# Index look-ups of 1024 columns, placed by a running count of two engines' work, in a fused attention and feed-forward kernel

## The chip, the cores and the metric

The kernel runs on one core of a Trainium2 chip. The metric is the device time of one execution in microseconds (us). Five engines work at the same time, each through its own queue in order: TensorE (PE), VectorE (DVE), ScalarE (ACT), GpSimd (POOL) and SyncE (SP). SP, ACT and POOL also issue DMA transfers.

## The reference

The input x has 2 x 2048 rows of 512 numbers. Two sublayers follow each other, each with a layer norm in front and a residual sum behind.

```python
q, k, v = x @ Wq, x @ Wk, x @ Wv             # attention between the 512 features, not the rows
w = softmax(q.T @ k / 4)                     # 512 x 512 for each of the two batches
x = x + (w @ v.T).T @ Wo                     # (x here stands for the normed x)

gate = x @ lut[gate_idx].T                   # 1376 x 512 weights, each one of 16 numbers
up   = x @ lut[up_idx].T
x = x + (silu(gate) * up) @ lut[down_idx].T
```

The weights of gate, up and down are given as indices 0 to 15 into a table of 16 numbers, and have to be looked up on the chip.

## The kernel before

All products are in float32. PE runs them in six stages one after the other: the Gram matrices of the normed x (L467), the 512 x 512 matrix chain of the attention with Strassen-like products of halves (L620), the product y of every 128 rows with that chain (L783), gate and up (L1008, tiles `a_g`, `b_g`, `c_g`, `w_g`, `x_g`, `z_g`), the last 96 of the 1376 rows (L1286), and down (L1008, tiles `a_d`, `b_d`, `c_d`). The order of PE, ACT, DVE and SP is the order of the program's text; a scheduler places the POOL instructions alone.

**Gate and up.** The 1376 hidden rows are eleven tiles `f` (0 to 10, the last has 96 rows). Every tile from 0 to 9 is multiplied with four pairs `p` of 512-column chunks: a `GateUp(f, p)` is one unit. From f = 2 on, units go by a `role`: `2 * (f % 2) + p % 2`, since products of two neighbouring tiles and two neighbouring pairs share work. A unit's stages on PE are `a1`, `c1`, `a2`, `c2`, `b`, `a3` and `a4`; `Line.run` runs the unit's `a4` late, inside the next unit. The PSUM tiles `a` and `c` have two buffers, the others one. Of a unit of role 2 (odd f, even p), DVE's last reading of the tile `a` is the addition in `a4` that makes `h1`; the unit after next begins with `a1` in the same buffer.

**The left sums.** For every even f, before the second pair's products, DVE makes sums of 128 columns of the weights of f and f + 1 (`sums_left`, tiles `lc`, `lb`, `ld`, four additions each).

**The look-ups.** A `Job` looks up 512 columns of indices: `fetch` loads them (POOL queue, two buffers), `cast` copies them to 16 bits on ACT, and `ops` runs 19 DVE instructions: three tests of a bit in 16 bits (L271, L272, L277), one shift of the indices (L275), eight picks between two table entries (L285) and seven `copy_predicated` that merge them by the bits (L297). There are 33 jobs: gate, up and down, eleven each. `ops` is a generator that yields an estimated cost after each instruction. `pump(us)` takes steps from it until the given time is spent, and is called at fixed places between PE's stages (`between`), in gate and up with a time that depends on the role:

```python
pace[0] = {0: 0.85, 1: 1.4, 2: 1.0, 3: 0.6}.get(u.role, 1.07)
```

Finished gate and up tiles are followed by four additions of 256 columns (`of_both`). Down's weights stay in SBUF in `wd` (the first six tiles) and `wd2` (the other five, which are looked up while PE already runs down's first part).

## Time and profile before

| | |
|---|---|
| median of 3 runs | 1064.85 us (1064.7 to 1065.43) |
| the profiled execution, its own time | 1064.8 us |
| its span in the profile | 1063.0 us |
| granted clock of TensorE, mean | 0.999 |
| instructions | 11592 |
| busy PE, DVE, ACT, POOL | 1057.0, 837.3, 385.0, 105.4 us |
| moved by DMA | 189.07 MB |

"Busy" is the time in which an engine ran at least one instruction. A record of a matmul is longer than the distance to the next matmul, since they are pipelined: matmuls of 512 columns have records of 592 ns and start 429 ns apart, and a float32 product has two of them. "Idle before, releaser" in a group or a line is the time for which an engine stood still ahead of an instruction, and what ended it.

### The profile page before, as it was taken

The page shows a single profiled execution, that of the slowest core. Times are in us where ns is not written, and L with a number is a line of the kernel's source. Part 1 is how long each engine was busy: PE and PEld are TensorE (multiplying, and loading weights), DVE is VectorE, ACT ScalarE, POOL GpSimd, SP SyncE. Part 2 cuts the span into 40 slices and gives each one's busy share as a digit, 9 for nine tenths or more (in the row PEclk, how much of TensorE's full clock was granted, in tenths as well). Part 3 has the DMA queues.
Part 4 walks back from the last instruction along what each step waited for, and adds up shares of the span by engine and source line. Part 5 has one row for each costly group of instructions (what it writes and reads, how often), then busy time and mean ns, then how long its engine had stood idle before and what let it go on. Part 6 is the DMA issues. An engine that isn't in the chain of part 4 may idle for free.

```text
span 1063.0 us, 11592 instructions
## 1 busy us (share of the span) xinstructions
PE 1057.0 (99%) x3554; PEld 661.0 (62%) x3554; DVE 837.3 (79%) x1842; ACT 385.0 (36%) x741; POOL 105.4 (10%) x160
## 2 busy tenths in 40 slices
PE   9999999999999999999999999999999999999998
PEld 5668887444444444444444444444998888888887
DVE  7878778889985889899699999964549998656554
ACT  4652532455532234444443444444223322211111
POOL 0000000011110120230041023013000000000000
PEclk9999999999999999999999999999999999999999
DMA  8750314499661365795597679569546675666773
GB/s 341 240 170 11 85 27 100 110 237 224 163 183 50 119 238 189 176 218 184 186 206 197 216 165 225 182 196 198 151 119 226 200 232 175 200 199 205 228 217 124
DMA packets 127710, 189.07 MB, mean 178 GB/s; under 512 B 18832, under 2 KB 59024, under 8 KB 126752
## 3 DMA queue, kind: packets, MB, share of 16 engines
q1 hardware_dynamic: 74528, 100.17, 29.9%
q0 software_dynamic: 15776, 39.92, 17.7%
q10 hardware_dynamic: 37344, 48.24, 14.0%
q8 instruction: 28, 0.46, 0.2%
q14 instruction: 34, 0.28, 0.1%
HBM read 108.60 MB, written 79.69 MB: 177 GB/s over the span
## 4 chain that ended last, share of the span: by engine, by line
PE 91%; DVE 4%; ACT 2%; DMA 1%; issue 1%; ACTq 1%; SPq 0%; DVEq 0%
PE a_g L1008 22%; PE a_d L1008 14%; PE y L783 10%; PE c_g L1008 8%; PE c_d L1008 7%; PE rows L1286 4%; PE b_d L1008 4%; PE x_g L1008 4%; PE z_g L1008 4%; PE w_g L1008 3%; PE b_g L1008 2%; PE ea_t L620 1%; PE ea_p L620 1%; PE ea_m L620 1%; DVE st_a L161 1%; PE gp L467 1%
## 5 line engine op out<-in xcount | busy, mean ns | idle before, releaser
L783 PE MATMUL y<-m,nT 128*128 128x512 f32 x256 | 110.2, 592 | 0.0
L783 PEld LDWEIGHTS y<-m,nT 128*128 128x128 f32 x256 | 48.6, 190 | 60.4 <-issue 57.4
L1008 PE MATMUL a_g<-xT_a,s 128*128 128x512 f32 x160 | 75.5, 594 | 0.0
L1008 PE MATMUL a_g<-xb,wg 128*128 128x512 f32 x160 | 75.3, 593 | 0.0
L1008 PE MATMUL c_g<-xb,wu 128*128 128x512 f32 x160 | 75.2, 592 | 0.0
L1008 PE MATMUL a_d<-dT,hs_a 128*128 128x256 f32 x288 | 72.6, 379 | 0.0
L467 PE MATMUL gp<-xn_a 128*128 128x128 f32 (+3 forms) x256 | 70.1, 434 | 0.7 <-ACT xn_a L239 0.7
L467 PEld LDWEIGHTS gp<-xn_a 128*128 128x128 f32 x256 | 43.9, 190 | 28.2 <-issue 15.1
L1008 PEld LDWEIGHTS a_d<-dT,hs_a 128*128 128x128 f32 x288 | 54.5, 189 | 7.7
L297 DVE COPY_PREDICATED wd<-b_wd,wd 128x512 f32<-128x512 int16 (+1 forms) x77 | 56.3, 732 | 1.3
L1008 PE MATMUL a_g<-xT_sq,s 128*128 128x512 f32 x120 | 56.7, 595 | 0.0
L1474 ACT COPY p_d<-a_d 128x256 f32<-128x256 f32 x32 | 11.9, 372 | 120.3 <-PE a_d L1008 120.3
L1008 PEld LDWEIGHTS a_g<-xb,wg 128*128 128x128 f32 x160 | 30.2, 190 | 38.8 <-issue 33.2
L1008 PEld LDWEIGHTS a_g<-xT_a,s 128*128 128x128 f32 x160 | 30.1, 190 | 38.9 <-issue 36.4
L1008 PEld LDWEIGHTS c_g<-xb,wu 128*128 128x128 f32 x160 | 30.4, 190 | 38.3 <-issue 38.0
L143 DVE TENSOR_TENSOR r<-r,p_d 128x256 f32<-128x256 f32 x64 | 26.9, 421 | 28.2 <-ACT p_d L1474 17.4
L285 DVE TENSOR_SCALAR wd<-idx_wd,lut_x,lut_sb 128x512 int32<-128x512 int32 (+1 forms) x88 | 45.9, 539 | 0.0
L1063 ACT COPY u<-a_g 128x512 f32<-128x512 f32 x40 | 23.4, 585 | 62.0 <-PE a_g L1008 59.6
L143 DVE TENSOR_TENSOR u<-c_g,u 128x512 f32<-128x512 f32 x40 | 27.5, 688 | 21.0 <-PE c_g L1008 15.5
L143 DVE TENSOR_TENSOR r<-r,a_d 128x256 f32<-128x256 f32 x64 | 26.6, 416 | 20.6 <-PE a_d L1008 20.6
L1286 PEld LDWEIGHTS rows<-last,xb 128*128 128x128 f32 x256 | 41.7, 190 | 0.5 <-issue 0.5
L1286 PE MATMUL rows<-last,xb 128*128 128x192 f32 x256 | 41.8, 326 | 0.0
(345 smaller groups left out, 2207.9 us busy)
## 6 DMA issues: line engine op xcount, KB each, us to landing
hd<-h SPq DMA_DIRECT2D x80, 256.0 KB, 3.3
h<-hd SPq DMA_DIRECT2D x40, 512.0 KB, 6.1
nl<-nd SPq DMA_DIRECT2D x32, 256.0 KB, 5.7
xnd<-xn_f ACTq DMA_DIRECT2D x16, 512.0 KB, 5.4
fl<-xnd POOLq DMA_DIRECT2D x32, 256.0 KB, 6.4
xn_back<-xnd SPq DMA_DIRECT2D x32, 256.0 KB, 3.8
rd<-r SPq DMA_DIRECT2D x32, 256.0 KB, 3.3
r<-rd SPq DMA_DIRECT2D x32, 256.0 KB, 4.0
```

The source lines that it names most:

```text
L143: nc.vector.tensor_tensor(dest, a, b, ALU.add)
L161: nc.vector.bn_stats(st, block)
L285: vec.tensor_scalar(dest.bitcast(I32), idx, lut_x[:rows, k : k + 1], lut_i[:rows, at : at + 1], ALU.bitwise_and, ALU.bitwise_xor,)
L297: vec.copy_predicated(dest, masks[level - 1], t)
L467: nc.tensor.matmul(gp[b][i][:, i * P :], xn[:, i, j % 2, :], xn[:, i:, j % 2, :], start=c % CPB == 0 and j == 0, stop=c % CPB == CPB - 1 a ...
L620: nc.tensor.matmul(ps[:, m, :], self.a[a][:, k, m * P : (m + 1) * P], self.b[b][:, k, :], start=first and m == k == 0, stop=k == 1, skip_g ...
L783: nc.tensor.matmul(ys[k], nTs[k][:, i, :], m[:, i, :], start=(i == 0), stop=(i == KB - 1))
L1008: nc.tensor.matmul(ps, lhsT, rhs, start=first and i == 0, stop=i == len(pairs) - 1, skip_group_check=not first,)
L1063: nc.scalar.copy(self.u2, self.a)
L1286: nc.tensor.matmul(ps[:, jj, :], x[:, j * P : (j + 1) * P], w, start=i == 0, stop=i == len(pairs) - 1,)
L1474: nc.scalar.copy(p1, self.a)
```

## The change

- A job looks up up to 1024 columns: gate and up of one tile together (`pair_job`), and two tiles of down together (`down_job`). There are 17 jobs in place of 33. The indices have one buffer in place of two; the fetch of the next job stands after the sixteenth step of a job (`LEAVES`, its last reading of the indices), and the cast of the next job after its last step.
- All of down's weights are looked up before PE starts down; each result is written to DRAM (`wdd`, on SP's queue) and read back: the first six tiles into two free rooms at the start of the stage of the last rows, the other five at the start of down.
- The weights of gate and up have four buffers in place of three (`w`), their sums three in place of two (`s`), the moving sums `tt` eight in place of nine.
- In gate and up, the last rows and down, a `Clock` adds up at build time the PE time of the matmuls and the DVE time of the additions; `fill(lead)` takes look-up steps until DVE's count is `lead` us ahead of PE's (1.4 in gate and up, 0.7 in down, -0.5 ahead of `a4` in a unit of role 3). In the stages ahead of gate and up, `pump` stays.
- The left sums of f = 4, 6 and 8 are made in the unit before, (f - 1, 3), one of the three tiles at each `between`. For role 2, the addition of `w_g` to `y` moves from `a4` to `first`.

The matmuls, their operands' values and their order are the same. The core of the diff:

```diff
+    class Clock:
+        pe = dve = 0.0
+        def matmul(self, cols):
+            self.pe += (4 * cols / 2.4 + 5) / 1000
+        def vector(self, cols, *of):
...
+            self.dve += 0.15 + 1.05 * cols / 1000
...
     class Job:
         def fetch(self, queue=nc.gpsimd):
-            self.idx = gub.tile([P, 512], I32, tag="idx", name=f"idx_{self.name}", bufs=2)[
...
+            t = gub.tile([P, 2, 512], I32, tag="idx", name=f"idx_{self.name}", bufs=1)
+            self.idx = self.part(t)
+            for i, of in enumerate(self.loads):
+                queue.dma_start(self.idx[:, i, :], of)
...
+        def after():
+            nc.sync.dma_start(wdd[:rows, i : i + k, :], made[0])
+            yield 0.1
...
             for k, cost in enumerate(job.ops()):
                 yield cost
-                if k == 9 and i + 1 < len(jobs):
-                    jobs[i + 1].cast()
-            if i + 2 < len(jobs):
-                jobs[i + 2].fetch()
+                if k == LEAVES and i + 1 < len(jobs):
+                    jobs[i + 1].fetch()
+            if i + 1 < len(jobs):
+                jobs[i + 1].cast()
+                yield 0.9
+
+    LEAVES = 15
...
+    def fill(lead):
+        while clock.dve < clock.pe + lead:
+            cost = step()
+            if cost is None:
+                clock.dve = max(clock.dve, clock.pe)
+                return
+            clock.dve += 1.1 * cost
...
         def first(self):
...
+            if self.role == 2:
+                add(self.y, of_d.ps, self.y)
...
             u.a2()
-            self.between()
             if role == 3:
+                self.between(-0.5)
                 last_a4()
+            else:
+                self.between()
...
         if sums_of and sums_of[0][0].ready(sums_of[0][1] | 1):
             next_sums_left()
         elif todo:
             todo.pop(0)()
-            pump(0.3)
-        else:
-            pump(pace[0])
+        fill(leads[0] if lead is None else lead)
...
-        if f > 1 and f % 2 == 0 and p == 0:
+        if (f, p) == (2, 0):
             sums_of += [(o, f) for o in seconds]
-        while p and sums_of:
+        if 2 < f < NFT - 2 and f % 2 and p == NPR - 1:
+            sums_of += [(o, f + 1) for o in seconds]
+        while f % 2 == 0 and p and sums_of:
             next_sums_left()
...
+    for q, (tag, n) in enumerate((("sq1", 4), ("a3", 2))):
+        t = room(tag, f"wd_{tag}")[:, :n, :]
+        nc.sync.dma_start(t, wdd[:, 4 * q : 4 * q + n, :])
...
+                nc.sync.dma_start(wd2[0][:, : NFT - K1 - 1, :], wdd[:, K1 : NFT - 1, :])
+                nc.sync.dma_start(wd2[0][:LAST, NFT - K1 - 1, :], wdd[:LAST, NFT - 1, :])
```

More of the change, by code (lines that the diff above doesn't have):

```diff
@@ L109, in tile_attn_ffn @@
     small = ctx.enter_context(tc.tile_pool(name="small", bufs=3))
-    wdp = ctx.enter_context(tc.tile_pool(name="wdp", bufs=1))
     dram = ctx.enter_context(tc.tile_pool(name="dram", bufs=1, space=DRAM))
@@ L118, in tile_attn_ffn @@
     K1 = 6
-    wd = wdp.tile([P, K1, E], F32, tag="wd", name="wd")
+    wdd = dram.tile([P, NFT, E], F32, tag="wdd", name="wdd")
     nd = dram.tile([NCH, P, KB, J, P], F32, tag="nd", name="nd")
@@ L137, in tile_attn_ffn, with made, copied, reset @@
     xnp = tc.alloc_tile_pool(name="xnp", bufs=1, side="right")
+    class Clock:
+        pe = dve = 0.0
+        there = {}
+        def matmul(self, cols):
+            self.pe += (4 * cols / 2.4 + 5) / 1000
+        def made(self, t):
+            self.there[id(t)] = (self.pe, t)
+        def copied(self, dest, t):
+            if id(t) in self.there:
+                self.there[id(dest)] = (self.there[id(t)][0] + 0.6, dest)
+        def vector(self, cols, *of):
+            for t in of:
+                if id(t) in self.there:
+                    self.dve = max(self.dve, self.there[id(t)][0])
+            self.dve += 0.15 + 1.05 * cols / 1000
+        def reset(self):
+            self.pe = self.dve = 0.0
+            self.there.clear()
+    clock = Clock()
+    def tensor(dest, a, b, op):
+        cols = 1
+        for n in dest.shape[1:]:
+            cols *= n
+        clock.vector(cols, a, b)
+        nc.vector.tensor_tensor(dest, a, b, op)
     def sub(dest, a, b):
-        nc.vector.tensor_tensor(dest, a, b, ALU.subtract)
+        tensor(dest, a, b, ALU.subtract)
     def add(dest, a, b):
-        nc.vector.tensor_tensor(dest, a, b, ALU.add)
+        tensor(dest, a, b, ALU.add)
+    def evict(dest, a):
+        nc.scalar.copy(dest, a)
+        clock.copied(dest, a)
     class Norm:
@@ L246, in tile_attn_ffn, with __init__, part @@
     class Job:
-        def __init__(self, name, rows, cols, load, dest, after, gate):
+        def __init__(self, name, rows, cols, loads, dest, after, gate):
             self.name, self.rows, self.cols = name, rows, cols
-            self.load, self.dest, self.after, self.gate = load, dest, after, gate
+            self.loads, self.dest, self.after, self.gate = loads, dest, after, gate
+        def part(self, t):
+            return t[: self.rows, : len(self.loads), : self.cols]
         def fetch(self, queue=nc.gpsimd):
-            self.idx = gub.tile([P, 512], I32, tag="idx", name=f"idx_{self.name}", bufs=2)[
-                : self.rows, : self.cols
-            ]
-            self.load(queue, self.idx)
+            t = gub.tile([P, 2, 512], I32, tag="idx", name=f"idx_{self.name}", bufs=1)
+            self.idx = self.part(t)
+            for i, of in enumerate(self.loads):
+                queue.dma_start(self.idx[:, i, :], of)
@@ L257, in cast, with bits @@
         def cast(self):
-            self.b3 = self.bits("b3", 2)
-            nc.scalar.copy(self.b3, self.idx)
-        def bits(self, tag, bufs):
-            t = gub.tile([P, 512], I16, tag=tag, name=f"{tag}_{self.name}", bufs=bufs)
-            return t[: self.rows, : self.cols]
+            self.b1 = self.bits("b1")
+            nc.scalar.copy(self.b1, self.idx)
+        def bits(self, tag):
+            t = gub.tile([P, 2, 512], I16, tag="b", name=f"{tag}_{self.name}", bufs=3)
+            return self.part(t)
@@ L265, in ops @@
         def ops(self):
-            rows, f, idx, b3 = self.rows, self.cols / 1024, self.idx, self.b3
+            rows, f, idx, b1 = self.rows, len(self.loads) * self.cols / 1024, self.idx, self.b1
             vec = nc.vector
             w = self.dest()
-            b1, b2 = self.bits("b1", 1), self.bits("b2", 1)
-            vec.tensor_scalar(b1, b3, 2, None, ALU.bitwise_and)
-            vec.tensor_scalar(b2, b3, 4, None, ALU.bitwise_and)
-            yield 0.2 + 0.54 * f
+            b2, b3 = self.bits("b2"), self.bits("b3")
@@ L275, in ops @@
+            vec.tensor_scalar(b2, b1, 4, None, ALU.bitwise_and)
+            yield 0.15 + 0.24 * f
+            vec.tensor_scalar(b3, b1, 8, None, ALU.bitwise_and)
+            yield 0.15 + 0.24 * f
+            vec.tensor_scalar(b1, b1, 2, None, ALU.bitwise_and)
+            yield 0.15 + 0.24 * f
             vec.tensor_scalar(idx, idx, 31, 31, ALU.logical_shift_left, ALU.arith_shift_right)
-            yield 0.1 + 0.55 * f
-            vec.tensor_scalar(b3, b3, 8, None, ALU.bitwise_and)
-            yield 0.1 + 0.27 * f
+            yield 0.15 + 0.48 * f
@@ L288, in pick @@
                     )
-                    yield 0.2 + 0.55 * f
+                    yield 0.25 + 0.48 * f
                     return
@@ L292, in pick @@
                 half = 1 << (level - 1)
-                t = gub.tile(
-                    [P, 512], F32, tag="pick", name=f"{self.name}_{level}_{at}", bufs=3
-                )[:rows, : self.cols]
+                t = self.part(gub.tile(
+                    [P, 2, 512], F32, tag="pick", name=f"{self.name}_{level}_{at}", bufs=3
+                ))
                 yield from pick(level - 1, at + half, t)
                 vec.copy_predicated(dest, masks[level - 1], t)
-                yield 0.1 + 1.17 * f
+                yield 0.18 + 0.96 * f
             yield from pick(4, 0, w)
@@ L307, in tile_attn_ffn, with pair_job @@
     ended = [0]
-    def gate_job(f):
+    def pair_job(f):
         f0, rows = FT[f]
         n = KB * rows
-        def load(queue, idx):
-            queue.dma_start(idx, gate_idx[:, KB * f0 : KB * f0 + n])
+        made = []
         def dest():
-            t = wgu.tile([P, KB, P], F32, tag="wg", name=f"wg_{f}", bufs=3)
-            gw[f] = t.rearrange("p k r -> p (k r)")[:, :n]
-            return gw[f]
+            made.append(wgu.tile([P, 2, KB * P], F32, tag="w", name=f"w_{f}", bufs=4)[:, :, :n])
+            return made[0]
         def after():
-            gw[f] = gw[f].rearrange("p (k r) -> p k r", k=KB)
-            yield 0.1
-        return Job(f"g{f}", P, n, load, dest, after, lambda: f < 3 + passed[0])
-    def up_job(f):
-        f0, rows = FT[f]
-        n = KB * rows
-        up = []
-        def load(queue, idx):
-            queue.dma_start(idx, up_idx[:, KB * f0 : KB * f0 + n])
-        def dest():
-            t = wgu.tile([P, KB, P], F32, tag="wu", name=f"wu_{f}", bufs=3)
-            up.append(t.rearrange("p k r -> p (k r)")[:, :n])
-            return up[0]
-        def after():
-            uw[f] = up[0].rearrange("p (k r) -> p k r", k=KB)
+            for to, i in ((gw, 0), (uw, 1)):
+                to[f] = made[0][:, i, :].rearrange("p (k r) -> p k r", k=KB)
             if f < NFT - 1:
-                deferred.append((lambda: f < 2 + ended[0], of_both()))
+                deferred.append((lambda: f < 3 + ended[0], of_both()))
             yield 0.1
@@ L347, in of_both @@
             g, u = gw[f], uw[f]
-            t = wgu.tile([P, 3, 2, P], F32, tag="s", name=f"s_{f}", bufs=2)
+            t = wgu.tile([P, 3, 2, P], F32, tag="s", name=f"s_{f}", bufs=3)
             a11, a12, a21, a22 = g[:, 0:2, :], g[:, 2:4, :], u[:, 0:2, :], u[:, 2:4, :]
@@ L351, in of_both @@
             for op, d, v, w in (
-                (add, s1, a21, a22), (sub, s2, s1, a11), (sub, a21, a11, a21), (sub, s4, a12, s2)
+                (ALU.add, s1, a21, a22), (ALU.subtract, s2, s1, a11),
+                (ALU.subtract, a21, a11, a21), (ALU.subtract, s4, a12, s2),
             ):
-                op(d, v, w)
+                nc.vector.tensor_tensor(d, v, w, op)
                 yield 0.42
             gu[f] = {"11": a11, "12": a12, "S3": a21, "22": a22, "S1": s1, "S2": s2, "S4": s4}
-        return Job(f"u{f}", P, n, load, dest, after, lambda: f < 3 + ended[0])
+        loads = [idx[:, KB * f0 : KB * f0 + n] for idx in (gate_idx, up_idx)]
@@ L360, in down_job, with dest @@
+        return Job(f"w{f}", P, n, loads, dest, after, lambda: f < 4 + ended[0])
     def down_job(i):
         f0, rows = FT[i]
-        return Job(
-            f"wd{i}", rows, E, lambda queue, idx: queue.dma_start(idx, down_idx[f0 : f0 + rows, :]),
-            lambda: wd_block(i)[:rows], lambda: iter(()), lambda: i < K1 or wd2,
-        )
+        k = 2 if i + 1 < NFT else 1
+        made = []
+        def dest():
+            if i < K1:
+                t = xnp.tile([P, 2, E], F32, tag="wds", name=f"wd_{i}", bufs=1)
+            else:
+                t = wgu.tile([P, 2, E], F32, tag="w", name=f"wd_{i}", bufs=4)
+            made.append(t[:rows, :k, :])
+            return made[0]
@@ L367, in tile_attn_ffn @@
+        def after():
+            nc.sync.dma_start(wdd[:rows, i : i + k, :], made[0])
+            yield 0.1
+        loads = [down_idx[f0 + P * q : f0 + P * q + rows, :] for q in range(k)]
+        turn = NFT + (i - K1) // 2
+        return Job(f"wd{i}", rows, E, loads, dest, after, lambda: i < K1 or turn < 4 + ended[0])
     wd2 = []
+    wd1 = []
     def wd_block(i):
-        return wd[:, i, :] if i < K1 else wd2[0][:, i - K1, :]
-    jobs = [job(f) for f in range(2) for job in (gate_job, up_job)]
@@ L374, in tile_attn_ffn @@
-    jobs += [down_job(i) for i in range(4)]
-    for f in range(2, NFT - 1, 2):
-        jobs += [gate_job(f), up_job(f), gate_job(f + 1), up_job(f + 1)]
-        jobs += [down_job(i) for i in {6: (4,), 8: (5,)}.get(f, ())]
-    jobs += [gate_job(NFT - 1), up_job(NFT - 1), *(down_job(i) for i in range(K1, NFT))]
-    assert len(jobs) == 3 * NFT
+        return wd1[i] if i < K1 else wd2[0][:, i - K1, :]
+    jobs = [pair_job(0), pair_job(1), down_job(0), down_job(2)]
+    for f in range(2, NFT - 1):
+        jobs.append(pair_job(f))
+        if f == 2:
+            jobs.append(down_job(4))
@@ L381, in looked_up @@
+    jobs += [pair_job(NFT - 1), *(down_job(i) for i in range(K1, NFT, 2))]
+    assert len(jobs) == NFT + (NFT + 1) // 2
     def looked_up():
@@ L387, in looked_up @@
                 job.cast()
+                yield 0.9
             for k, cost in enumerate(job.ops()):
                 yield cost
-                if k == 9 and i + 1 < len(jobs):
-                    jobs[i + 1].cast()
-            if i + 2 < len(jobs):
-                jobs[i + 2].fetch()
+                if k == LEAVES and i + 1 < len(jobs):
+                    jobs[i + 1].fetch()
+            if i + 1 < len(jobs):
+                jobs[i + 1].cast()
+                yield 0.9
+    LEAVES = 15
     lookup = looked_up()
@@ L426, in tile_attn_ffn @@
         nc.sync.dma_start(xc[c], xr[c])
-    jobs[1].fetch(nc.sync)
     def load_weight(src, tag, name):
@@ L765, in turn @@
     def turn(to, t):
+        clock.vector(CH)
         nc.vector.transpose(to.rearrange("p m (t b) -> p m t b", b=Q), t)
@@ L898, in __init__ @@
             self.name, self.tag, self.weights, self.operand = name, tag, weights, operand
-            self.right, self.far, self.parts = {}, {}, {}
+            self.right, self.left, self.far, self.parts = {}, {}, {}, {}
         def sums(self, g):
@@ L925, in ready @@
         def ready(self, f):
-            return f in gu if self is of_d else f in gw and len(gw[f].shape) == 3 and f in uw
+            return f in gu if self is of_d else f in uw
         def sums_left(self, f):
@@ L933, in sums_left @@
             s1, s2, s3, s4 = (t[:, q, :] for q in range(4))
-            self.left = {"22": a22, "S1": s1, "S2": s2, "S3": s3, "S4": s4}
+            self.left[f] = {"22": a22, "S1": s1, "S2": s2, "S3": s3, "S4": s4}
             return [
@@ L943, in pair @@
             else:
-                left = self.left[a]
+                left = self.left[u.f & ~1][a]
             return [(left, self.right[u.p // 2][b])]
@@ L976, in back @@
             return t
-    RT, TT = 3, 9
+    RT, TT = 3, 8
     def in_two(t):
@@ L1007, in mm @@
         for i, (lhsT, rhs) in enumerate(pairs):
+            clock.matmul(rhs.shape[-1])
             nc.tensor.matmul(
@@ L1011, in mm @@
             )
+        clock.made(ps)
     class GateUp:
@@ L1042, in a1 @@
                 self.p1 = self.temp("p1")
-            nc.scalar.copy(self.p1, self.a)
+            evict(self.p1, self.a)
             of_b.add_part(self, self.p1)
@@ L1057, in c1 @@
             self.p7 = self.temp("p7")
-            nc.scalar.copy(self.p7, self.c)
+            evict(self.p7, self.c)
         def a2(self):
@@ L1062, in a2 @@
             self.u2 = self.temp("u2", bufs=2)
-            nc.scalar.copy(self.u2, self.a)
+            evict(self.u2, self.a)
             of_c.add_part(self, self.u2)
@@ L1115, in b @@
                 mm(self.p1, of_b.pair(self, "12", "21"), False)
-                nc.scalar.copy(h0, of_b.ps)
+                evict(h0, of_b.ps)
                 add(h0, self.p1, h0)
@@ L1141, in first @@
                 add(self.u2, self.c, self.u2)
-            nc.vector.tensor_tensor(self.h0, self.h0, self.u2, ALU.mult)
+            tensor(self.h0, self.h0, self.u2, ALU.mult)
             self.store(self.h0, 2 * self.p)
+            if self.role == 2:
+                add(self.y, of_d.ps, self.y)
         def a4(self):
@@ L1150, in a4 @@
                 of_d.begin(self, "11", "11")
-                nc.scalar.copy(h1, of_d.ps)
+                evict(h1, of_d.ps)
                 mm(self.a, of_d.pair(self, "12", "21"), False)
@@ L1155, in a4 @@
                 of_d.go_on(self, "S4", "22")
-                nc.scalar.copy(h1, of_d.ps)
+                evict(h1, of_d.ps)
                 add(h1, self.a, h1)
@@ L1160, in a4 @@
                     mm(self.a, of_d.pair(self, "22", "T4"), False)
-                    add(self.y, of_d.ps, self.y)
                 add(h1, self.a, self.y)
@@ L1169, in out @@
         def out(self):
-            nc.vector.tensor_tensor(self.h1, self.h1, self.c22, ALU.mult)
+            tensor(self.h1, self.h1, self.c22, ALU.mult)
             self.store(self.h1, 2 * self.p + 1)
@@ L1203, in run @@
             u.a2()
-            self.between()
             if role == 3:
+                self.between(-0.5)
                 last_a4()
+            else:
+                self.between()
             u.extra2()
@@ L1238, in __init__ @@
         def __init__(self):
-            s = [wgu.tile([P, 3, 2, P], F32, tag="s", name=f"last_{i}", bufs=2) for i in range(2)]
-            flat = [
-                t.rearrange("p a b c -> p (a b c)").rearrange("p (k r) -> p k r", k=KB) for t in s
-            ]
-            self.w, self.v = flat
+            self.w, self.v = (
+                wgu.tile([P, 3, 2, P], F32, tag="s", name=f"last_{i}", bufs=3)
+                .rearrange("p a b c -> p (a b c)").rearrange("p (k r) -> p k r", k=KB)
+                for i in range(2)
+            )
         def copied(self):
@@ L1285, in products @@
                 for i, (x, w) in enumerate(pairs):
+                    clock.matmul(r)
                     nc.tensor.matmul(
@@ L1305, in rows @@
                 nc.sync.dma_start(hrd[c], self.h)
-    pace = [1.0]
     sums_of = []
@@ L1310, in tile_attn_ffn, with between @@
     todo = []
-    def between():
+    leads = [1.4]
+    def between(lead=None):
         if to_load:
@@ L1473, in a1 @@
             p1 = self.temp("p1")
-            nc.scalar.copy(p1, self.a)
+            evict(p1, self.a)
             self.onto(0, 0, p1)
@@ L1480, in c1 @@
             p7 = self.temp("p7")
-            nc.scalar.copy(p7, self.cc)
+            evict(p7, self.cc)
             self.onto(1, 1, p7)
@@ L1486, in a2 @@
             u2 = self.temp("u2")
-            nc.scalar.copy(u2, self.a)
+            evict(u2, self.a)
             self.onto(1, 0, u2)
@@ L1540, in ops @@
             op()
-            pump(max(0.0, pace[0] - 0.75))
         return ops
@@ L1548, in tile_attn_ffn @@
     line = Line(between)
+    clock.reset()
     for (f, p), following in zip(units, units[1:] + [(NFT, 0)]):
         while f not in gu or f > 1 and p and not all(o.ready(f | 1) for o in seconds):
-            step()
+            clock.dve += step()
         assert p in xs
-        if f > 1 and f % 2 == 0 and p == 0:
+        if (f, p) == (2, 0):
             sums_of += [(o, f) for o in seconds]
-        while p and sums_of:
+        if 2 < f < NFT - 2 and f % 2 and p == NPR - 1:
+            sums_of += [(o, f + 1) for o in seconds]
+        while f % 2 == 0 and p and sums_of:
             next_sums_left()
@@ L1567, in tile_attn_ffn @@
         u = GateUp(f, p)
-        pace[0] = {0: 0.85, 1: 1.4, 2: 1.0, 3: 0.6}.get(u.role, 1.07)
         line.run(u)
@@ L1579, in tile_attn_ffn @@
                     in_place.append(last)
-    assert not todo and next(lookup, None) is None
+    assert not todo
     x2p.release()
@@ L1586, in tile_attn_ffn @@
     h = Hidden(0, 0)
+    for q, (tag, n) in enumerate((("sq1", 4), ("a3", 2))):
+        t = room(tag, f"wd_{tag}")[:, :n, :]
+        nc.sync.dma_start(t, wdd[:, 4 * q : 4 * q + n, :])
+        wd1 += [t[:, i, :] for i in range(n)]
     todo += by_two(last_rows.weights() + down_sums(0, hps["dT"]))
@@ L1605, in tile_attn_ffn @@
     todo.clear()
-    pace[0] = 0.75
+    while step() is not None:
+        pass
+    assert next(lookup, 0) == 0
+    clock.reset()
+    leads[0] = 0.7
     parts = [(part, c) for part in range(2) for c in range(NCH)]
@@ L1619, in tile_attn_ffn @@
                 wd2.append(wdq.tile([P, NFT - K1, E], F32, tag="wd2", name="wd2"))
+                nc.sync.dma_start(wd2[0][:, : NFT - K1 - 1, :], wdd[:, K1 : NFT - 1, :])
+                nc.sync.dma_start(wd2[0][:LAST, NFT - K1 - 1, :], wdd[:LAST, NFT - 1, :])
             if (part, c, jj) == (0, NCH - 1, 0):
-                while step() is not None:
-                    pass
                 todo += by_two(down_sums(1, wdq))
```

## The prediction

> **What bounds the kernel now.** I read the engines' totals first, then what PE waited for, then the groups of the look-ups, then the timeline at the places where PE stood.

> ```profile
> PE 1057.0 (99%) x3554; PEld 661.0 (62%) x3554; DVE 837.3 (79%) x1842; ACT 385.0 (36%) x741; POOL 105.4 (10%) x160
> ...
> PE 91%; DVE 4%; ACT 2%; DMA 1%; issue 1%; ACTq 1%; SPq 0%; DVEq 0%
> ```

> The second line is the chain that ended last. PE is the bound in every stage, and the change takes no matmul away. So a faster DVE is worth only the time that PE stands for it. That time is small: all distances between PE's starts, less 429, 323, 216, 162 or 110 ns for 512, 384, 256, 192 or 128 columns, leave 7.6 us. 4.3 lie in the first 70 us (the first records at half the clock, then the first norms), 0.85 in the attention, 2.2 in gate and up, none to speak of in the last rows and down. The change could win at most some 3 us.

> The stretches show how loaded DVE is in gate and up (columns: span, then busy time of PE, PEld, DVE, ACT, POOL):

> ```profile
> 384.00:748.50 364.50, 364.14 (x846) 159.15 (x845) 311.58 (x606) 155.93 (x273) 71.00 (x93) 1.00 0.73 198
> ```

> DVE is busy 311.6 of 364.5 us. It has 15% of slack on average, and the order inside its queue decides whether PE feels it. Two places where PE did:

> ```profile
> 393.84 0.28 DVE L143 TENSOR_TENSOR lc<-wu 128x128 f32<-128x128 f32 x1
> ...
> 394.51 0.30 PEld L1008 LDWEIGHTS z_g<-T_c_in,lc 128*128 128x128 f32 x2 [1.02 <-DVE lc L140]
> 394.51 1.13 PE L1008 MATMUL z_g<-T_c_in,lc 128*128 128x512 f32 x2 [0.19 <-DVE lc L140]
> ```
> ```profile
> 563.72 0.68 DVE L143 TENSOR_TENSOR y<-w_g,y 128x512 f32<-128x512 f32 x1
> ...
> 564.50 0.69 DVE L143 TENSOR_TENSOR h<-a_g,y 128x512 f32<-128x512 f32 x1
> ...
> 565.24 0.30 PEld L1008 LDWEIGHTS a_g<-xb,wg 128*128 128x128 f32 x2 [0.85 <-DVE h L143]
> 565.24 1.55 PE L1008 MATMUL a_g<-xb,wg 128*128 128x512 f32 x3
> ```

> In the first, a product waits for left sums. In the second, the next unit's `a1` waits for the buffer of `a`, which DVE frees with the addition that makes `h1` at the end of a role 2 unit. The second is the place that matters below.

> **The look-ups get cheaper, off the path.** The forms of 384 and 512 columns give the slope:

> ```profile
> L285 DVE TENSOR_SCALAR g<-idx_g,lut_x,lut_sb 128x512 int32<-128x512 int32 x70 | 36.0, 537 | 0.0
> ...
> L297 DVE COPY_PREDICATED g<-b_g,g 128x512 f32<-128x512 int16 x40 | 29.4, 734 | 1.0
> ...
> L285 DVE TENSOR_SCALAR g<-idx_g,lut_x,lut_sb 128x384 int32<-128x384 int32 x7 | 3.1, 473 | 0.0
> ...
> L297 DVE COPY_PREDICATED g<-b_g,g 128x384 f32<-128x384 int16 x4 | 2.4, 589 | 0.1
> ```

> A pick costs 537 - 473 = 64 ns per 128 columns, so 1024 take 0.537 + 4 x 0.064 = 0.79 us; a merge 0.145 per 128, so 1.31. The bit tests (0.285 at 512, 0.25 at 384) come to 0.42, the shift (0.42, 0.35) to 0.70. A whole job: 8 x 0.79 + 7 x 1.31 + 3 x 0.42 + 0.70 = 17.4 us, against 2 x (8 x 0.537 + 7 x 0.734 + 3 x 0.285 + 0.42) = 21.4. Some 16 pairs save about 4 us each, 63 us of DVE's 837. The casts on ACT fall from 33 of 0.62 us to 17 of about 0.92. None of it is PE's time. [...]

> **What goes from the path.** Four waits in the units after the left sums (0.46 at 393.7, 0.16 at 498.2, 0.41 at 579.5, 0.26 at 671.1, restarts included): two behind the sums themselves, two behind an ACT copy that had queued behind DVE. With four weight buffers and the sums a unit earlier they are ready: -1.3. The wait at 564.6 (0.29) goes, since `y` is added earlier: -0.3. What is late next is the subject of the following part.

> **What comes onto the path: the buffer of `a`.** I take a role 2 unit, f odd. From the end of its `a3` to the moment when its buffer is wanted again, PE runs the role 3 unit: `a1`, `c1`, `a2` with 4 matmuls each, the late `a4` with 2, `a3` with 4: 18 x 0.429 = 7.72 us (in the trace 557.25 to 564.96 for f = 5, p = 2). DVE learns of the end of `a3` 0.2 us later (`p` copied at 559.17 after PE went on at 558.97) and PE needs 0.06 to see the last addition. So DVE has 7.46 us for everything in its queue from `c22` to `h1`. In the trace an independent addition of 512 columns follows after 0.60, a dependent one after 0.72, four left sums take 0.93, and other records overlap their successor by 0.09.

> The new order puts this into it:
> - five additions (two of `u2`, `h0`, `y`, `h1`): 0.72 + 0.72 + 0.61 + 0.75 + 0.69 = 3.5, and `c22` 0.60: 4.1 us always.
> - f = 5, p = 0: two bit tests, the shift, two picks, a merge: records 4.43, less six overlaps 0.54, and up to three waits on the predecessor of 0.13: 3.9 to 4.3. With 4.1: 8.0 to 8.4, late by 0.5 to 0.95.
> - f = 3 and 5, p = 2: one pick 0.70, one merge 1.22, and the twelve left sums that now stand here, 2.8: with 4.1, 8.5 to 8.8, late by 1.05 to 1.3, each.
> - f = 7, p = 0 (768 columns: picks 0.66, merges 1.02): four picks and two merges, 4.1 to 4.4: late by 0.8 to 1.1. f = 7, p = 2: two merges 1.86 and left sums 2.8: late by 0.95 to 1.2.
> - f = 9, p = 0: two merges and two picks, 3.8 to 4.0: late by 0.45 to 0.65.
> - f = 3, p = 0: one merge and four additions of 256 columns, 1.22 + 1.45: 6.8, in time. f = 9, p = 2 has little left to look up, in time.

> The rule of the planner says the same: after `c1` of the role 3 unit it lets DVE be 1.4 us ahead, then come five additions of 3.5; the buffer is wanted 4 + 2 + 4 matmuls, 4.3 us, after `c1`. Six waits sum to 4.8 to 6.5 us, and each restart costs another 0.10 (the first matmul of a product after a wait starts 533 ns ahead of the next, not 429). I take the middle: 5.7 + 0.6 = +6.3.

> **The rest.** The matmuls' order is unchanged: 0. Down's weights through DRAM: 2.75 MB written and read, under 3% of the 189 MB. SP's queue holds the first two writes between the loads of `nl`; those wait for DVE jobs that end a chunk, 13.7 us of PE, ahead: 0, or up to 0.5. The first 1.5 MB come back when the last pair of f = 9 ends; DVE's sums of them stand behind three others in the last rows, where DVE was busy 19.1 of 41.5 us and PE has four PSUM tiles in rotation: 0, up to 0.5. Behind this read on SP stand the last stores of `hd`, wanted by nobody soon. In down DVE loses the look-ups of 797 to 900; PE did not wait there: 0. The larger steps make the attention's and the product stage's pumps coarser: between -0.85 (its waits all go) and +1.0; the stages are tight in the same way, so +0.3. The eight `tt` tiles in place of nine hold back one load of three per pair, needed a unit later: 0.

> **The index buffer.** Fetch, landing and cast now stand in a row. A fetch is followed by three merges (3.6 us) before its cast is due on ACT. Two issues of 0.55 and a landing of 3 to 4.1 us (medians of the idx rows) make the cast wait 0.5 to 1.6; ACT's next copy has about 2 us until PE wants it (the buffer of `a` is wanted 2.6 us after `a1` at the earliest, the copy takes 0.6). So 0. [...]

> **Rivals.**
> 1. Not slower: the DVE queue comes out short enough. It decides in the role 3 units from the point where the stretch is under 7.46 us, 1.0 to 1.3 less than my sums for p = 2. For it: DVE as a whole is 63 us lighter, and the wait of 564.6 is 0.29 only. Against: the order is fixed and five 512-column additions and twelve left sums have durations that the trace shows. Time: 1064.8 - 1.6 = 1063.2, or 1062.4 if the attention's waits go too. 13%.
> 2. The index buffer binds. If the idx loads land like `fl` on the same queue (6.4 us) ACT is late by 6.4 + 1.1 - 3.6 - 2.0 = 1.9 us, nine times in gate and up: +17 us on top, 1087. For it: one idx_wd load took 7.5. Against: medians of 3 to 4. 5%.

> **The numbers.** The profiled execution took 1064.8 us, 1.8 more than its span, and the median of the runs is 1064.85, so the sum is made on 1064.8: - 1.6 + 6.3 + 0.3 = 1069.8. This has 82%. The range reaches from 1065.5 (half of the waits do not come, no loss elsewhere) to 1073 (all waits at their upper ends, 7.1, and 1 us more in each of the attention and the down stage); rivals 1 and 2 are left out, 18%. What this measurement can tell from no change is about 0.2%, 2.1 us: rival 1 is mostly within it (10%, and 3% faster), the low edge of the main case adds 2%. Faster 3%, same 12%, slower 85%.

> **What would show it.** In the profile after: the bit tests, picks and merges at about 0.42, 0.79 and 1.31 us for 1024 columns, DVE busy near 775 us; PE's busy time within 1 us of before outside of waits; PE waiting for DVE `h` ahead of `a_g` six times, 0.5 to 1.3 us each, at the starts of (4,0), (6,0), (8,0), (5,2), (7,2), (9,2); no more wait for `lc`. I am wrong if those waits are missing, or if ACT's casts wait for DMA by more than 2 us each.

## The result, and the profile after

The changed kernel takes 1070.99 us, the median of four runs (1070.88 to 1071.78). The kernel before, beside it on the same chip, took 1065.03 us. The ratio is 1.0057 with a 95% interval of 1.0040 to 1.0075. It is slower by 6 us. The profiled execution took 1070.93 us with a span of 1069.1, where that of before took 1064.8 with 1063.0.

The engines' totals of the changed kernel:

```profile
PE 1057.3 (99%) x3554; PEld 660.8 (62%) x3554; DVE 804.0 (75%) x1538; ACT 384.3 (36%) x725; POOL 106.1 (10%) x160
...
PE 37%; DMA 1%; issue 1%; POOL 0%; DVE 0%; ACT 0%; POOLq 0%; ACTq 0%
```

PE has the same 3554 matmuls and the same busy time, yet the span is 6 us longer. DVE has 33 us less to do. The chain that ended last could be followed back for some 40% of the span only, so it can't be compared with the 91% of before; the waits and the timeline have to do.

The stretch from 384 to 748.5 us (span, then busy PE, PEld, DVE, ACT, POOL):

```profile
384.00:748.50 364.50, 359.17 (x833) 156.92 (x832) 292.28 (x441) 153.72 (x261) 69.57 (x90) 1.00 0.72 195
```

DVE is 19 us less busy here than before (311.58), and still PE has lost 5 us (364.14). More slack on DVE went together with more waiting on PE. Whom PE waited for (us in total, times, longest):

```profile
PE a_g L1065 <- DVE h L172: 5.3, 6, 1.3
PE idle L502 <- POOL ident masks.py:199: 1.4, 1, 1.4
PE gp L522 <- DVE xn_a L223: 0.7, 1, 0.7
PE a_g L1065 <- ACT u L181: 0.4, 1, 0.4
```

The first line is new: six times a first product into `a` waits for the addition that makes `h1`. The waits for `lc` and `y` are gone. A wait counts from the moment when a modelled matmul ends; the distance between starts, less the usual 429 ns, is a little longer. By that measure the six are 1.47 us at 472.6, 0.92 at 546.4, 1.15 at 566.4, 1.12 at 639.9, 1.05 at 660.1 and 0.59 at 733.4, together 6.30, and 0.62 for six restarts.

One of them in the timeline, the start of (5, 2), DVE and PE as they came:

```profile
540.58 0.69 DVE L322 TENSOR_SCALAR idx_w<-idx_w 128x1024 int32<-128x1024 int32 x1
540.69 1.88 PE L1065 MATMUL c_g<-xb,w 128*128 128x512 f32 x4
541.30 1.53 DVE L330 TENSOR_SCALAR w<-idx_w,lut_x,lut_sb 128x1024 int32<-128x1024 int32 x2
542.41 1.88 PE L1065 MATMUL a_g<-xT_a,s 128*128 128x512 f32 x4
542.87 1.31 DVE L342 COPY_PREDICATED w<-b_w,w 128x1024 f32<-128x1024 int16 x1
544.08 0.67 DVE L172 TENSOR_TENSOR u<-z_g,u 128x512 f32<-128x512 f32 x1
...
546.18 0.68 DVE L172 TENSOR_TENSOR y<-w_g,y 128x512 f32<-128x512 f32 x1
546.96 0.69 DVE L172 TENSOR_TENSOR h<-a_g,y 128x512 f32<-128x512 f32 x1
547.71 0.70 PE L1065 MATMUL a_g<-xb,w 128*128 128x512 f32 x1 [0.76 <-DVE h L172]
```

Shift, picks and merge run back to back ahead of the additions. The last addition ends at 547.65 and PE goes on 0.06 us later. PE could have begun near 546.79.

A seventh wait had not been predicted. In the chain, followed back from 756 us (start, us, what):

```profile
744.29 6.76 DMA idx_wd<-in_down_idx_dram
...
751.13 0.07 ACT b_wd L303
...
751.65 0.58 ACT u L181
752.24 0.04 issue
752.28 1.98 PE a_g L1065 x4
```

The indices of down's last rows landed 6.76 us after their issue. Their cast stood on ACT for them, the copy of `u` stood behind the cast, and PE needed the bank that this copy frees: 0.57 us and 0.10 for the restart.

### The profile page after: what moved, and what is told of

The parts are those of the page before. It is cut to its first block, busy times and chain, and to the rows that moved or that the text cites. A ratio compares the mean times of both kernels' runs of the same rounds, so it can differ in the third digit from the quotient of the medians.

```text
span 1069.1 us, 11338 instructions
## 1 busy us (share of the span) xinstructions
PE 1057.3 (99%) x3554; PEld 660.8 (62%) x3554; DVE 804.0 (75%) x1538; ACT 384.3 (36%) x725; POOL 106.1 (10%) x160
## 5 line engine op out<-in xcount | busy, mean ns | idle before, releaser
L342 DVE COPY_PREDICATED w<-b_w,w 128x1024 f32<-128x1024 int16 (+1 forms) x77 | 98.7, 1282 | 1.4
L1065 PE MATMUL a_g<-xb,w 128*128 128x512 f32 x160 | 75.9, 597 | 5.3 <-DVE h L172 5.3
L1065 PE MATMUL c_g<-xb,w 128*128 128x512 f32 x160 | 75.2, 592 | 0.0
L330 DVE TENSOR_SCALAR w<-idx_w,lut_x,lut_sb 128x1024 int32<-128x1024 int32 (+1 forms) x88 | 67.6, 793 | 0.2
L1065 PEld LDWEIGHTS a_g<-xb,w 128*128 128x128 f32 x160 | 29.8, 190 | 45.9 <-issue 33.0
L1065 PEld LDWEIGHTS c_g<-xb,w 128*128 128x128 f32 x160 | 30.4, 190 | 38.3 <-issue 38.0
L342 DVE COPY_PREDICATED wd<-b_wd,wd 128x1024 f32<-128x1024 int16 (+1 forms) x42 | 50.6, 1206 | 0.8
L172 DVE TENSOR_TENSOR c<-a_g,p 128x512 f32<-128x512 f32 x40 | 27.6, 689 | 23.2 <-PE a_g L1065 22.0
```

The source lines that it names most:

```text
L172: nc.vector.tensor_tensor(dest, a, b, op)
L330: vec.tensor_scalar(dest.bitcast(I32), idx, lut_x[:rows, k : k + 1], lut_i[:rows, at : at + 1], ALU.bitwise_and, ALU.bitwise_xor,)
L342: vec.copy_predicated(dest, masks[level - 1], t)
L1065: nc.tensor.matmul(ps, lhsT, rhs, start=first and i == 0, stop=i == len(pairs) - 1, skip_group_check=not first,)
```

## The experiments

Two theories were set against each other. The first: PE waits for the buffer of `a`, since look-ups and left sums stand in the DVE queue between `c22` and `h1`. The second: something else in the change costs the time (DVE as a whole, the place of the `y` addition, the single index buffer).

**e1: fewer look-ups in role 3 units.**

```diff
-            self.between()
+            self.between(LATE if role == 3 else None)      # LATE = -0.7; after a1 and after c1
```

> The changed kernel, with look-up steps held back in units of role 3: DVE's lead there is -0.7 us in place of 1.4 after a1 and c1. Theory (DVE's queue between c22 and h1 is too long for the 7.46 us that PE leaves): with no look-up step in it the stretch is 4.1 us for p = 0 and 6.9 with the left sums for p = 2, so the three waits at p = 0 (0.92, 1.12, 0.59 and 0.10 each) vanish and those at p = 2 fall from 1.47, 1.15, 1.05 to 0.5 or less each: 1070.9 - 6.9 + 0.5 = 1064.5 us. Rival (DVE is overloaded in gate and up as a whole): the steps held back come due in the units of role 0 to 2, and PE waits there for as long: 1069 to 1071 us.

Measured: 1066.43 us, ratio to the kernel before 1.0013 (1.0003 to 1.0022). Three waits went ((5, 2), (7, 2), (9, 2)); those of (4, 0), (6, 0) and (8, 0) stayed, at 1.07, 1.56 and 1.48 us, where I had expected 0.5 or less each. So the time is 1.9 us over the expectation. DVE's timeline ahead of the first of these:

```profile
468.47 0.28 DVE L172 TENSOR_TENSOR lb<-w,lb 128x128 f32<-128x128 f32 x1
469.76 0.69 DVE L172 TENSOR_TENSOR u<-z_g,u 128x512 f32<-128x512 f32 x1 [1.00 <-DMA u<-part_r_c]
...
471.89 0.68 DVE L172 TENSOR_TENSOR y<-w_g,y 128x512 f32<-128x512 f32 x1
472.49 0.28 DVE L172 TENSOR_TENSOR ld<-s 128x128 f32<-128x128 f32 x1
...
473.42 0.68 DVE L172 TENSOR_TENSOR h<-a_g,y 128x512 f32<-128x512 f32 x1
```

DVE stood idle for 1.00 us until a DMA onto `u` had landed; then the sums of `ld` (0.93 us) went in front of `h1`. The stretch has two limits, DVE's work and this landing. Where the second holds, taking look-ups away from before it brings nothing. In the changed kernel, too, DVE stood 0.22 us at 470.10 for this landing, ahead of the wait of (4, 0).

**e2: the left sums back in (f, 0).**

```diff
-        if (f, p) == (2, 0):
+        if f > 1 and f % 2 == 0 and p == 0:
             sums_of += [(o, f) for o in seconds]
-        if 2 < f < NFT - 2 and f % 2 and p == NPR - 1:
-            sums_of += [(o, f + 1) for o in seconds]
```

> The changed kernel, with the left sums of f = 4, 6, 8 made in unit (f, 0) again. Theory: the sums lc and lb are counted by the planner, which puts look-up steps in their place up to the same lead; only ld (0.93 us) stands behind its last filling. The three waits at p = 2 fall by 0.9 each, those at p = 0 stay: 1070.9 - 2.8 = 1068.1 us, and up to 0.8 more if the waits for left sums of the kernel before return. Rival (the moved left sums are the whole cause at p = 2): the three waits vanish with 4.0 us: 1066.9 us. Rival (look-ups alone): nothing changes, 1070.9 us.

Measured: 1072.52 us, 1.0070 (1.0055 to 1.0085). This missed, by two things. The planner fills up to its lead: without the sums it put more look-ups into the same place, so (4, 0) still waited 1.47, and (6, 0) came down to 0.58 only. And the look-ups came out shifted in time, so that near 658 us a cast stood for its indices as at 751 in the changed kernel, with `u` behind it. PE stood 2.1 us, and then ran slowly (columns as above; the figure after POOL's is the granted clock):

```profile
655.00:660.00 5.00, 3.49 (x9) 1.22 (x7) 3.56 (x6) 1.73 (x3) 0.86 (x1) 1.00 1.01 267
660.00:661.00 1.00, 0.56 (x1) 0.34 (x2) 0.05 (x1) 1.00 (x3) 0.32 (x1) 0.82 0.08 29
661.00:662.00 1.00, 1.00 (x2) 0.34 (x1) 0.64 (x1) 0.43 (x1) 1.00 (x2) 0.50 0.06 16
662.00:663.00 1.00, 1.00 (x3) 0.34 (x2) 0.00 (x0) 0.00 (x0) 0.12 (x1) 0.50 0.95 53
663.00:664.00 1.00, 1.00 (x3) 0.48 (x2) 0.00 (x0) 0.00 (x0) 0.00 (x0) 0.50 0.84 152
```

From 660.44 on, four matmuls started 853 ns apart in place of 429, 1.7 us more. The wait and its aftermath cost 3.8 us.

**e5: as e2, that one cast put off.** (Told here, as it tests the reading of e2.)

```diff
             if i + 1 < len(jobs):
+                if jobs[i + 1].name == "wd6":
+                    yield None
                 jobs[i + 1].cast()
```

> The kernel with the left sums back, and the cast of one look-up (rows of down, the one that landed at 658.8) put off by one stretch between products. Theory: that cast stood on ACT for its indices, the copy of `u` behind it, and PE with it for 2.1 us; after so long a stand the next four matmuls ran at 853 ns instead of 429, 1.7 us more. Without it: 1072.5 - 3.8 = 1068.7, and no matmul of 853 ns after 10 us. Rival (the left sums' old place itself costs that): 1072.5 again, with a wait at another place near 658.

Measured: 1069.37 us, 1.0039 (1.0024 to 1.0055). The wait near 658 and the slow matmuls were gone; of the 0.7 us over the expectation, a wait for the last rows' cast (0.28 and 0.10, at 749.7) is 0.4. (8, 0) no longer waited and (6, 0) only 0.60, together 1.7 us less than in the changed kernel. So the old place of the sums itself had cost nothing: what e2 lost was the index buffer's.

**e3: e1 and e2 together.**

> The changed kernel, with both: lead -0.7 in units of role 3, and the left sums in (f, 0) again. Theory: the stretch from c22 to h1 is 4.1 us everywhere, none of the six waits is left: 1070.9 - 6.9 = 1064.0 us, plus up to 0.8 for returning waits for left sums. Rival (overload as a whole): 1069 us or more.

Measured: 1064.46 us, 0.9995 (0.9985 to 1.0004). As expected: of the six waits, 0.29 and 0.16 us are left, and here the cast near 655 did not hold PE up. So of the 6.9 us of the six waits 0.66 are left with their restarts, and what stands in the DVE queue of the role 3 units, look-ups and left sums together, made the rest; taking away either alone (e1, e5) is not enough.

**e4: the kernel before, with the addition to `y` in `first`.**

```diff
             self.store(self.h0, 2 * self.p)
+            if self.role == 2:
+                add(self.y, of_d.ps, self.y)
```

> The kernel before, with one edit: for role 2 the addition of w_g to y stands in first() in place of a4. Theory: the wait of 0.29 us at 564.6 goes and the waits for left sums stay, PE's waits in gate and up fall from 2.2 to 1.9 us: 1064.6 us, which the time alone does not tell from 1064.9. Rival (the earlier y delays h0 and its store, or u2): a new wait of up to 0.6 us in units of role 3.

Measured: 1065.16 us (one run), where the kernel before had a median of 1065.16. The wait of 564.6 went, that of 498.2 too, and one of 0.96 us at 655.8 came in their place, a wait for DVE `h` at the start of (8, 0). By distances between PE's starts, gate and up lost 0.6 us more than in the kernel before. The expected 0.3 us did not come, and the new wait is of the rival's kind, longer than its 0.6. Alone, then, the move brings one wait for the buffer of `a`; it is not what costs the 6 us.

**e9: another bank for `a`.** The sharpest test: DVE's work and order stay, and what PE waits for is taken away. `b` is a PSUM tag that units of role 2 do not use.

```diff
-            self.a = self.view("a")
+            self.a = self.view("b" if self.role == 2 and self.p == 2 else "a")
```

> The changed kernel, DVE's work and order untouched, but `a` of the role 2 units with p = 2 lies in the PSUM bank of tag `b`, which nobody uses there. So the unit after a role 3 unit finds a buffer of `a` that was free long ago. Theory (PE waits for nothing but that buffer): the six waits and their restarts go, 6.3 + 0.6 = 6.9 us: 1071.0 - 6.9 = 1064.1, or 0.7 less if the cast at 751 also falls elsewhere. Rival (DVE is late as such, and the next work that needs it waits instead): a part comes back at the banks of `x` or `c` or at the copy into `p1`, 1066 or more.

Measured: 1065.08 us, 0.9999 (0.9990 to 1.0008). All six waits are gone. PE and then DVE at the start of (5, 2):

```profile
543.88 1.96 PE L1065 MATMUL a_g<-xT_a,s 128*128 128x512 f32 x4
545.68 1.88 PE L1065 MATMUL b_g<-xb,w 128*128 128x512 f32 x4
```
```profile
545.09 0.68 DVE L172 TENSOR_TENSOR y<-w_g,y 128x512 f32<-128x512 f32 x1
545.87 0.69 DVE L172 TENSOR_TENSOR h<-a_g,y 128x512 f32<-128x512 f32 x1
```

The addition still ends 0.9 us after PE's next product has begun, as late as ever, and nobody waits. The 1.0 us over the expectation is the seventh wait: the copy of `u` behind the last cast now held PE for 1.71 us, not 0.57.

**e10: e9, and the last cast put off** (as in e5, with `wd10`).

> As e9, and the cast of the last rows of down put off by one stretch between products, so that the copy of `u` at 751 doesn't stand behind a cast that waits for its indices (0.57 + 0.10 us). Theory: 1063.4. Rival (the wait only moves): 1064.1.

Measured: 1063.77 us, 0.9987 (0.9978 to 0.9995). PE's waits in the whole execution:

```profile
PE idle L504 <- POOL ident masks.py:199: 1.4, 1, 1.4
PE gp L524 <- DVE xn_a L223: 0.8, 1, 0.8
PE ea_s L677 <- ACT a L698: 0.3, 1, 0.3
```

None is listed in gate and up. This version beats the kernel before by 0.13%, and its median lies 7.2 us below that of the changed kernel.

**e8: e3, and `y` loaded behind `u`.** The load of `y` waits on the POOL queue for DVE, and the DMA onto `u` stood behind it.

```diff
-            if self.role in (2, 3):
+            if self.role == 3:
                 self.y = of_d.back(self)
...
+        def late_y(self):                        # called after a2, ahead of a4
+            self.y = of_d.back(self)
+            add(self.y, of_d.ps, self.y)
```

> The kernel with both edits (fewer look-ups in role 3 units, left sums back), and in role 2 units the load of `y` issued after that of the next unit's `u` on the GpSimd queue, so that `u` no longer stands behind a load that waits for DVE. In the run of both edits DVE stood 1.0 to 1.5 us for that load of `u`, and PE then waited 0.29 at 473.1 and 0.16 at 655.9. Theory: the load of `u` lands about 0.9 us sooner, both waits go with their restarts, 0.65 us: 1063.8, and PE waits nowhere in role 3 units. Rival (the landing is set by the queue's transfers, not by its place): 1064.5, the same waits.

Measured: 1064.16 us, 0.9990 (0.9981 to 0.9999). The DMA onto `u` landed 0.9 us earlier (DVE began with it at 469.21, not 470.13), the wait at 473 went and that at 655.9 shrank from 0.16 to 0.11. The mechanism is right. The difference from e3, 0.3 us, is within what the runs can tell.

**e11: e9, the left sums back, `y` behind `u`.**

> As e9, with the left sums back in the units that use them and the load of `y` behind that of `u`, but the look-ups still filled into the role 3 units. Theory: with the free buffer neither place of the sums nor the filling matters; no wait in the role 3 units, 1063.5 to 1064.1, beside at most one cast that stands for its indices (0.5 to 3.8). Rival (the stretch of role 3 is still too long for something): 1066 or more.

Measured: 1069.82 us (1067.32 to 1072.56), 1.0043 (1.0026 to 1.0060). No wait for `h1`, as the theory says. But both late casts held the copy of `u` again: PE stood 2.89 us at 653.6, with 1.7 us of slow matmuls behind it, and 0.48 at 749.4. I had allowed for one such cast, with 0.5 to 3.8; the expectation held for its mechanism and missed in the time.

**e7: the cast two merges earlier.**

```diff
-            if i + 1 < len(jobs):
-                jobs[i + 1].cast()
-                yield 0.9
+                if k == LEAVES + 1 and i + 1 < len(jobs):
+                    jobs[i + 1].cast()
+                    yield 0.9
```

> The changed kernel with the next cast queued after one merge instead of after all three that follow the fetch: 2.4 us of DVE work less between fetch and cast. It doses the single index buffer. In gate and up the casts began 6.7 to 15 us after their fetch, four of them 6.7 to 7.9 us after it. Theory: those four become late by up to 2.4 us, and where ACT's next copy is late by more than its slack, PE stands 0.5 to 2 us: 1074 to 1081. Rival (ACT has slack enough, the buffer costs nothing wherever the cast stands): 1071.

Measured: 1100.63 us, 1.0330 (1.0316 to 1.0344). What ACT's casts waited for:

```profile
ACT b_w L303 <- DMA idx_w<-in_up_idx_dram: 25.9, 7, 12.4
ACT b_wd L303 <- DMA idx_wd<-in_down_idx_dram: 19.9, 5, 7.1
```

Twelve of seventeen casts waited, 45.8 us in all, where the changed kernel has one such line with 1.7 us (its stand at 751 is put down to DVE there, which had long been done). I had expected 3 to 10 us more, and it was 30. Two stands of 9.6 and 5.0 us do the largest part of it, with another 2.9 and 2.6 us for the half-speed matmuls behind them. In DVE's work the edit takes 2.4 us from between fetch and cast. In time it takes more, since the merges are put in between products: in the changed kernel the cast of `wd6` began 14.1 us after the second issue of its fetch (651.76 and 665.83), and here it stood on ACT from 0.8 us after it (673.43 and 674.22), for the 7.1 us of the second line. The 12.4 us of the first line have one more cause. The fetch stood on the POOL queue behind four loads of `fl`, and these waited 9.4 us for the writing of `xnd`; so it was issued at 311.87, when its cast had stood on ACT since 306.4.

**e6 and e12: the width of the look-ups.** Picks and merges as two of 512 columns, in the changed kernel (e6) and in e10 (e12).

```diff
-                    vec.tensor_scalar(
-                        dest.bitcast(I32), idx, ...
+                    for i in range(len(self.loads)):
+                        vec.tensor_scalar(
+                            dest[:, i, :].bitcast(I32), idx[:, i, :], ...
```

> The changed kernel with every pick and merge issued as two of half the columns, all else alike. Starts of back-to-back instructions lie 446 and 623 ns apart at 512 columns, 717 and 1195 at 1024: a job costs DVE 8 x 0.175 + 7 x 0.051 = 1.8 us more, 16 jobs 28, so DVE is busy near 832 us. Theory: PE feels it only where picks stand in the stretch from `c22` to `h1`: the six waits grow by 0.1 to 0.8, together 2.2, to 1073.2. Rival (DVE's load as a whole decides): more than 1080. Second rival (width is worth nothing on the path): 1071.0.

> The kernel of e10 with every pick and merge again as two of half the columns, as in e6: DVE busy near 826 us, 22 more than e10. Theory (with the buffer of `a` free, DVE's load is off the path): 1063.8 + at most 1.0 for the first norms and the attention, where e6 lost some 1.0 us: 1063.8 to 1065, and no wait for DVE `h`. Rival (the width itself brings PE's time also where no buffer binds): as much as between e6 and the changed kernel, 3.8 us: 1067.6.

Measured: e6 1074.78 us, 1.0089 (1.0075 to 1.0103); e12 1066.48 us, 1.0010 (1.0000 to 1.0020). PE's waits, of e6 and then of e12:

```profile
PE a_g L1067 <- DVE h L172: 6.9, 6, 1.5
PE gp L524 <- DVE xn_a L223: 1.7, 1, 1.7
PE a_g L1067 <- ACT u L181: 1.5, 1, 1.5
```
```profile
PE a_g L1069 <- ACT b_g L181: 1.3, 2, 0.7
PE gp L526 <- DVE xn_a L223: 0.4, 1, 0.4
```

DVE's busy time rose by 22 us in e6, to 826.0, where I had reckoned with 28, and PE felt 3.8. By distances of starts the six waits grew by 1.6 (6.30 to 7.86), the seventh by 1.1, the product stage by 0.7 and the first 70 us by 0.5. In e12, with the free buffer, no wait for `h` came, but 2.7 us did by the medians of e10 and e12 (2.4 by the distances), more than my 1.2 and less than the rival's 3.8. Two copies of `p1` into bank `b` now stood for the same late `h1`, 0.8 us each with their restarts 1.85 in all, and the product stage lost 0.7. So the wider forms are worth 2.4 to 3.8 us on PE's path, and freeing the buffer moved the deadline back by a unit's first copy; it did not take it away.

## Why the prediction was right

The forecast was 1069.8 us and slower; it came to 1071.0. By its steps, and by distances between PE's starts, which leave 13.4 us where before left 7.6:

- **The buffer of `a`: right, in every place.** Six waits at the six starts named. Predicted and measured: (4, 0) 1.05 to 1.3, 1.47; (5, 2) 0.5 to 0.95, 0.92; (6, 0) 1.05 to 1.3, 1.15; (7, 2) 0.8 to 1.1, 1.12; (8, 0) 0.95 to 1.2, 1.05; (9, 2) 0.45 to 0.65, 0.59. With restarts 6.9, where I took 6.3. e9 shows that the buffer is the cause, e1 and e3 that its lateness comes from what stands in the queue. The place most in error is (4, 0), by 0.17 over its range: there DVE stood 0.22 us for the DMA onto `u`, and the sum of the stretch had no landing in it.
- **What goes: right.** The four waits after the left sums and the one for `y` are gone, 1.6 us.
- **The forms: right; their saving: too large.** Measured medians are 0.426 (bit test), 0.804 (pick) and 1.306 (merge); predicted 0.42, 0.79, 1.31. (The cast took 1.04 us, predicted 0.92.) But DVE's busy time fell by 33 us and not 63. The term that failed is the job's sum of 17.4 against 21.4 us, made from durations. Records overlap: in the medians of those that follow each other without a stop, picks of 512 columns last 539 ns and start 456 apart, merges 734 and 626; at 1024 it is 804 and 722, 1306 and 1199. By starts a pair of 512 costs 2 x (8 x 0.456 + 7 x 0.626) = 16.1 in picks and merges, one of 1024 8 x 0.722 + 7 x 1.199 = 14.2: 1.9 saved, not 3.4. I had the overlap in the stretch's sum, and left it out here.
- **"None of it is PE's time": too simple.** e6 and e12 show 2.4 to 3.8 us of PE's time for some 22 us of DVE's, as look-ups stand ahead of additions with a deadline.
- **The rest, +0.3: small, as predicted, but by parts that cancel.** The step from the products to gate and up cost 0.37 more, the attention 0.15, and span and last matmul lie 0.3 us further apart, while the first 70 us came out 0.8 shorter. That this comes to about nothing is luck. DRAM round trip and `tt` cost nothing that the distances show.
- **The index buffer at nothing: wrong by 0.67 us as built, and near an edge that I did not see.** I took ACT's slack for sufficient with landings at their median. The landing that hurt took 6.76 us, and the wait falls or stays out with each small shift of the plan: 0.67 us here, none in e3, 1.8 in e9, 3.8 in e2, 30 in e7. Rival 2 had the mechanism right, and its price was one event, not nine.
- **Rival 1 (not slower)** had its condition in the stretch being under 7.46 us. It was met by none of the six.
- **The low edge** of 1065.5 does not follow from its own words: with half of the six waits and no other loss the sum is 1064.8 - 1.6 + 3.15 = 1066.3. The measured time lies inside the range with either edge.

Left open: a second index buffer in SBUF was not tried; so what the single one costs is known only by moving casts.

## What to carry to other kernels

Where one engine is the bound, look for the deadlines that other engines' queues have to it (a PSUM bank to be freed, a copy, a landing), and add up what stands in the queue ahead of each; total slack says little. A planner that fills up to a lead takes every gap that an edit opens, and a single buffer makes the schedule's small shifts visible, so undoing one part may miss for a reason that has nothing to do with that part. Before work is trimmed, see whether another bank can hold the tile: one line (e9) did what two scheduling edits (e3) did.
